# Graph attention on one core: the planner of the instruction order models two lines of transfers instead of one, with other durations and latencies

## The chip, the cores and the metric

The kernel runs on one core of a Trainium2 chip. The metric is the device time of one execution in microseconds (us). The engines that matter here are TensorE (matmuls, "PE" in the profile; "PEld" is its loading of weights), VectorE ("DVE"), ScalarE ("ACT"), GpSimd ("POOL") and SyncE ("SP"). SyncE only issues DMA transfers. GpSimd issues the accumulating transfers. Every engine works through its own list of instructions in order, and waits at the head of the list for semaphores of the others.

## What is computed

32 graphs of 512 nodes with 512 features each go through a layer norm with ReLU, two layers of graph attention (4 heads of 256, then one head of 512) and a residual:

```
h = relu(layernorm(x));  mask = (adj > 0) | eye
def gat(x, W, a_src, a_dst, bias):
    xl = (x @ W) per head
    e = leaky_relu(<xl, a_src>[source] + <xl, a_dst>[target], 0.2);  e = where(mask, e, -1e9)
    return einsum(softmax(e over sources), xl) + bias
out = x + gat2(elu(gat1(h)))
```

All data are float32; the masks inside the kernel are bfloat16.

## The kernel before, in words

**Tiles and stages.** A graph's 512 rows lie as four blocks of 128 partitions. A graph passes these stages: load of x in four blocks (`load`), load of adj and making of the mask (`masks`), layer norm (`norm`, `norm_turn`), projection of layer 1 (`project1`), attention weights of each head (`Soft.columns`, `first`, `second`), their product with the projected features (`gather1`), projection of layer 2 (`project2`), the attention of layer 2 in the same way (`second_layer`, `gather2`), and the store. Most products are done with seven half-size products in place of eight, so VectorE forms sums of blocks (`sums`, `sums1`, `sums2`) before a product and combines results after it. The main loop (line 1429) interleaves stages of several graphs.

**Transfers.** On SyncE's queue (issued at line 448 unless said): blocks of x and adj (256 KB each), the residual's x and the outputs (512 KB), the mask's copy to memory (dm<-m), the mask's transposes (mt<-m, line 603) and, for graphs from the third on, the transposes of normalised x (x<-adj, line 662). Each row of scores goes through memory: `lay` writes a small flipped block (drr<-flip, das<-flip) and `spread` reads it back to all partitions (rr<-drr, as<-das, up to 512 KB). On GpSimd's queue (line 453) the mask is added to the scores p by accumulating transfers (p<-dm, two of 512 KB for a head), and GpSimd also computes a power for the layer norm (line 622).

**A head's chain.** VectorE writes p from rr (four instructions, line 445), two accumulates add the mask, ScalarE takes exp of p (four instructions, line 442), VectorE forms sums of p, TensorE multiplies (line 459). There are three slots for p, two each for rr, as and adj. In `norm_turn`, ScalarE copies a block of x into a slot of adj (adj<-x), SyncE transposes it back into x (x<-adj), and ScalarE writes ht from it.

**The order.** Everything is first recorded as jobs (`Program.add`): engine, cost in us, keys that it reads and writes, and for a transfer its size in us of the memory path. `order` then makes a list schedule by a model of the engines. TensorE's jobs keep the order in which they were recorded; the order on the other four engines is what the planner chooses: each time the job that can start first, and among an engine's ready ones the one with the lowest rank. Ranks come from a pass from the end backwards (`backwards`), twelve rounds of backward and forward passes, and then a local search (`sooner`), which raises jobs that stand behind a modelled hole of TensorE. `emit` writes the instructions out in the order found. The modelled times are used for nothing else.

**Transfers in the model before.** There is one line of transfers for both queues. A transfer starts 0.8 us after its issue ends (`DMA_LEAD`) or when the line is free, takes its size, and its readers are released 2.0 us later (`DMA_TAIL`); SP and POOL are held while the line is over 3.5 us ahead (`AHEAD`):

```
landed = max(landed, t + jobs[j][1] + self.DMA_LEAD) + jobs[j][4]
r = landed + self.DMA_TAIL
```

The issue of a transfer costs 0.4 us on SP (1.3 for a transpose, 0.55 for a flip) and 0.95 on POOL.

Of the kernel before, what the change touches and what calls it, by code (L numbers as in the profile page):

```python
# [19 lines left out]
P = 128  # L20
# [80 lines left out]
class Program:  # L101
# [6 lines left out]

    CROSS, SAME = 0.15, 0.07
    PAIRS = {("PE", "ACT"): 0.21, ("PE", "DVE"): 0.21, ("DVE", "POOL"): 0.58, ("POOL", "DVE"): 0.4}  # L110
    DMA_LEAD, DMA_TAIL, AHEAD = 0.8, 2.0, 3.5

    def __init__(self):
        self.jobs, self.writer, self.readers = [], {}, defaultdict(list)
# [25 lines left out]
    def forwards(self, rank):  # L140

        jobs, after = self.jobs, self.after
        n = len(jobs)
        cause = [None] * n
        left = [len(job[2]) for job in jobs]
        ready_at, start, landed = [0.0] * n, [0.0] * n, 0.0
        free, soon, ready = defaultdict(float), defaultdict(list), defaultdict(list)
        tensor = deque(j for j in range(n) if jobs[j][0] == "PE")
        for j in range(n):
            if not left[j] and jobs[j][0] != "PE":  # L150
                heappush(soon[jobs[j][0]], (0.0, j))
        done = []
        while len(done) < n:
            j, t = self.next_job(rank, free, soon, ready, tensor, left, ready_at, landed - self.AHEAD)
            start[j] = t
            free[jobs[j][0]] = t + jobs[j][1]
            done.append(j)
            if jobs[j][4] is not None:
                landed = max(landed, t + jobs[j][1] + self.DMA_LEAD) + jobs[j][4]
            for s in after[j]:  # L160
                if jobs[j][4] is not None:
                    r = landed + self.DMA_TAIL
                else:
                    r = t + jobs[j][1] + self.latency(j, s)
                if r > ready_at[s]:
                    ready_at[s], cause[s] = r, j
                left[s] -= 1
                if not left[s] and jobs[s][0] != "PE":
                    heappush(soon[jobs[s][0]], (ready_at[s], s))
        return start, done, cause  # L170

    def sooner(self, rank, start, cause, span, gain, first, last):
# [16 lines left out]
    def backwards(self, rank):  # L189

        jobs = self.jobs
        n = len(jobs)
        left = [len(s) for s in self.after]
        ready_at, start, moving = [0.0] * n, [0.0] * n, 0.0
        free, soon, ready = defaultdict(float), defaultdict(list), defaultdict(list)
        tensor = deque(j for j in reversed(range(n)) if jobs[j][0] == "PE")
        found = [j for j in range(n) if not left[j]]
        todo = n
        while True:
            for j in found:  # L200
                if jobs[j][4] is not None:
                    moving = max(moving, ready_at[j]) + jobs[j][4]
                    ready_at[j] = moving + self.DMA_LEAD
                if jobs[j][0] != "PE":
                    heappush(soon[jobs[j][0]], (ready_at[j], j))
            if not todo:
                return start
            j, t = self.next_job(rank, free, soon, ready, tensor, left, ready_at)
            start[j] = t
            free[jobs[j][0]] = t + jobs[j][1]  # L210
            todo -= 1
            found = []
            for d in jobs[j][2]:
                later = self.DMA_TAIL if jobs[d][4] is not None else self.latency(d, j)
                ready_at[d] = max(ready_at[d], t + jobs[j][1] + later)
                left[d] -= 1
                if not left[d]:
                    found.append(d)

    def next_job(self, rank, free, soon, ready, tensor, left, ready_at, hold=0.0):  # L220

        best = None
        for e in ("PE", "ACT", "DVE", "POOL", "SP"):
            if e == "PE":
                if not tensor or left[tensor[0]]:
                    continue
                t = max(free[e], ready_at[tensor[0]])
            elif ready[e]:
                t = free[e]
            elif soon[e]:  # L230
                t = max(free[e], soon[e][0][0])
            else:
                continue
            if e in ("SP", "POOL"):
                t = max(t, hold)
            if best is None or t < best[0]:
                best = (t, e)
        t, e = best
        if e == "PE":
            return tensor.popleft(), t  # L240
        while soon[e] and soon[e][0][0] <= t:
            k = heappop(soon[e])[1]
            heappush(ready[e], (rank[k], k))
        return heappop(ready[e])[1], t

    ROUNDS = 12

    def order(self):
        jobs = self.jobs
# [5 lines left out]

        need, pe = [0.0] * n, None
        for j in reversed(range(n)):
            later = self.DMA_LEAD + self.DMA_TAIL + (jobs[j][4] or 0.0)
            need[j] = max(
                (  # L260
                    need[s] + jobs[s][1] + (later if jobs[j][4] is not None else self.latency(j, s))
                    for s in self.after[j]
                ),
                default=0.0,
            )
            if jobs[j][0] == "PE":
                if pe is not None:
                    need[j] = max(need[j], need[pe] + jobs[pe][1])
                pe = j
# [43 lines left out]
def tile_gat(  # L313
# [254 lines left out]
    def load(b):  # L568
        XT[b] = []
        for t in range(NT):  # L570
            xk, xt = xs.take()
            dma(0.75, (), [xk], xt, x[b, t * P : (t + 1) * P, :])
            XT[b].append((xk, xt))

    def masks(b):

        MASK[b] = mk, md = mds.take()
        tk, mt = mts.take()
        every = [("m", t) for t in range(2)]
        for g in range(2):  # L580
            for t in range(2):
                ak, a = adjs.take()
                row = (2 * g + t) * P
                dma(0.75, (), [ak], a, adj[b, row : row + P, :])
                dve(
                    0.34, [ak], [("m", t)], nc.vector.tensor_scalar,
                    m[:, t, :], a, 0.0, -BIG, op0=OP.is_le, op1=OP.mult,
                )
                adjs.give(ak)
            blocks = bass.AP(  # L590
                tensor=m.tensor, offset=m.offset + 2 * g * P, ap=[m.ap[0], [N + P, 2], [1, P]]
            )
            dve(
                0.3, every, every, nc.vector.tensor_max,
                blocks, blocks, diag[:, None, :].to_broadcast([P, 2, P]),
            )
            dma(
                0.25, every, [mk + (g,)],
                md[:, 2 * g : 2 * g + 2].rearrange("p t n -> p (t n)"), m.rearrange("p t n -> p (t n)"),
            )  # L600
            prog.add(
                "SP", 1.3, every, [tk + (g,)],
                lambda g=g: nc.sync.dma_start_transpose(
                    mt[:, 2 * g : 2 * g + 2].rearrange("p t d r -> p (t d) r"),
                    m.rearrange("p t n -> p (t n)"),
                ),
                1.25,
            )
        MASKT[b] = tk, mt

# [20 lines left out]
    def norm_turn(b, t):  # L631
# [19 lines left out]
        else:  # L651
# [10 lines left out]
                lambda: nc.sync.dma_start_transpose(  # L662
                    back.rearrange("p (g n) -> p g n", n=P), words
                ),
                1.27,
            )
            act(
                1.21, [xk], [("ht", t, 0), ("ht", t, 1)],
# [13 lines left out]
    class Soft:  # L682
# [7 lines left out]
        def lay(self, v, keys, rows, through, n=NT):  # L690
# [7 lines left out]
                f, bass.AP(tensor=v.tensor, offset=v.offset, ap=[v.ap[0], [1, k], [0, c]]),  # L698
            )
            dma(  # L700
                0.03, [fk], [dk], dr[:k].rearrange("k (b j) -> b k j", j=32),
                bass.AP(
                    tensor=f.tensor, offset=f.offset, ap=[[c * f.ap[0][0], P // c], [1, 32]]
                ),
# [5 lines left out]
        def spread(self, laid, to):  # L710

            dk, dr, rows, n, through = laid
            ok, o = to.take()
            dma(
                0.18 * rows * n, [dk], [ok], o[:, :rows, : n * P],
                bass.AP(tensor=dr.tensor, offset=dr.offset, ap=[[0, P], [n * P, rows], [1, n * P]]),
            )
            through.give(dk)
            return ok, o
# [73 lines left out]
        def second(self, h):  # L793
# [9 lines left out]
            for d0, d1, laid in self.rr.pop(h):  # L803
# [17 lines left out]
                if not here:  # L821
                    mk, md = MASK[self.b]
                    for us in (0, 1), (2, 3):
                        keys = p_keys(pk, us)
                        accumulate(
                            2.2, keys + [mk + (us[0] // 2,)], keys,
                            *(t[:, us[0] : us[-1] + 1].rearrange("p t n -> p (t n)") for t in (p, md)),
                        )
                for u in range(NT):
# [408 lines left out]
    def residual(b, places=(pair(ts_),) * 2):  # L1238

        XR[b] = []  # L1240
        for r in range(2):
            ks, xr, give = places[r]()
            halves = [*ks, *(("xr", b, r, c) for c in range(2))]
            if len(ks) == 1:
                halves += [ks[0] + (q,) for q in range(2)]
            dma(
                1.5, [x2_key(b, 0, 0)], halves, xr,
                x[b, r * 2 * P : (r + 1) * 2 * P, :].rearrange("(m p) f -> p m f", p=P),
            )
            XR[b].append((ks, halves, xr, give))  # L1250
# [29 lines left out]
    def gather2(b, soft, blocks, order=LAST):  # L1280
# [4 lines left out]
        def put(n, us, bks, ps, fresh):  # L1285
# [9 lines left out]
            if n == 4 or r == 0 and upper[0] == 0:  # L1295
                upper[0] = -1
                dma(
                    1.5, halves, halves,
                    out[b, r * 2 * P : (r + 1) * 2 * P, :].rearrange("(m p) f -> p m f", p=P), xt,
                )  # L1300
                give()
# [9 lines left out]
    def gather2_plain(b, soft):  # L1311
# [3 lines left out]
        for d in range(NT):  # L1315
# [9 lines left out]
            xr = xr[:, d % 2, :]  # L1325
            key = ("xr", b, d // 2, "d", d % 2)
            dve(0.6, [bk, *halves], [key], nc.vector.tensor_add, xr, ps, xr)
            dma(0.75, [key], (), out[b, d * P : (d + 1) * P, :], xr)
            banks.give(bk)
            yield  # L1330
        give_p(pk)
# [191 lines left out]
```

## Time and profile before

| | us |
|---|---|
| median of 3 runs | 2848.57 (2844.51 to 2850.7) |
| the profiled execution | 2833.14 |
| its span, first to last instruction | 2831.3 |
| TensorE busy | 2765.0 |
| VectorE busy | 2432.6 |
| ScalarE busy | 2389.0 |
| GpSimd busy | 327.3 |

The profile is of one execution. Busy times count the time in which an engine has an instruction in work; instructions of one engine overlap a little. In a line of the timeline stand the start, the duration, the engine, the line of the code, the operation, what it writes and reads (buffer numbers left out), the shapes and the number of instructions merged; in brackets the engine's idle time before it, and what ended that. In a line of waits stand the waiting engine and what it waited for, the total in us, the number of times and the longest. DMA share is the mean busy share of the 16 DMA engines; packets of the two queues that overlap on an engine count twice, so it can exceed 1. The granted clock is TensorE's, 1.00 being full speed.

### The profile page before, as it was taken

Reading aid. Unit: us, or ns where it says so; the run is one execution under the profiler, and the core shown is the slowest. Engines: PE = TensorE matmul, PEld = TensorE weight load, DVE = VectorE, ACT = ScalarE, POOL = GpSimd, SP = SyncE. Lnnn points to the kernel's source line nnn. Section 1 sums busy time; section 2 is a strip of 40 time slices with the busy share of each in tenths; the row PEclk is TensorE's granted clock in tenths of the full one; section 3 lists DMA queues with packets and bytes.
Section 4 is the critical chain, followed back from the end, with each engine's and each line's share of the span. In section 5 each row is a group of like instructions: output and inputs, shape, how many; then the busy total and the mean of one; then the engine's idle time right before and its main releaser. Section 6 shows DMA issues by size and latency. Waiting matters only on the chain. (4 is left out here: it accounts for less than half of the span.)

```text
span 2831.3 us, 39738 instructions
## 1 busy us (share of the span) xinstructions
PE 2765.0 (98%) x12524; PEld 2384.8 (84%) x12524; DVE 2432.6 (86%) x5526; ACT 2389.0 (84%) x4506; POOL 327.3 (12%) x356
## 2 busy tenths in 40 slices
PE   8899999999999999999999999999999999999998
PEld 6588888888888888887888878888888888888876
DVE  7788898897888988987888879898888888898885
ACT  5888888888888889887898878988988888888873
POOL 0101111110111101110011101111010111010110
PEclk9999999999999999999999999999999999999999
DMA  7656766668776667776678765677666877666753
GB/s 229 139 142 173 205 186 181 160 181 172 200 189 161 178 181 191 203 176 145 176 183 195 192 144 174 178 211 190 171 166 169 189 186 187 170 178 182 190 168 101
DMA packets 373830, 501.95 MB, mean 177 GB/s; under 512 B 220788, under 2 KB 225652, under 8 KB 373620
## 3 DMA queue, kind: packets, MB, share of 16 engines
q1 hardware_dynamic: 327828, 332.67, 43.0%
q0 software_dynamic: 45792, 166.74, 25.8%
q8 instruction: 99, 1.62, 0.2%
q14 instruction: 111, 0.91, 0.1%
HBM read 316.41 MB, written 51.31 MB: 130 GB/s over the span
## 5 line engine op out<-in xcount | busy, mean ns | idle before, releaser
L459 PE MATMUL mm<-w_sb,hs 128*128 128x257 f32 (+2 forms) x3032 | 695.7, 381 | 1.4 <-DVE hs L445 1.3
L459 PEld LDWEIGHTS mm<-w_sb,hs 128*128 128x128 f32 x3032 | 575.3, 190 | 86.6 <-DVE hs L445 3.8
L459 PE MATMUL mm<-w_sb,ht 128*128 128x258 f32 x2112 | 500.6, 382 | 5.2 <-DVE xl L445 2.4
L459 PE MATMUL mm<-p,xl 128*128 128x256 f32 (+1 forms) x1984 | 485.6, 388 | 20.0 <-ACT p L442 17.5
L445 DVE CUSTOM_DVE_ANT_1 l<-l,mt 128x512 f32<-128x512 f32 x640 | 424.6, 684 | 80.7 <-ACT l L442 75.7
L442 ACT ACTIVATE l<-l,low 128x512 f32<-128x512 f32 x640 | 455.1, 713 | 39.7 <-DVE low L445 37.9
L442 ACT ACTIVATE l<-as,z 128x512 f32<-128x512 f32 x640 | 433.9, 711 | 59.0 <-DMA as<-das 58.3
L442 ACT ACTIVATE p<-p,z 128x512 f32<-128x512 f32 (+1 forms) x636 | 426.9, 709 | 66.8 <-DMA p<-dm 53.1
L453 POOL DMA_DIRECT2D p<-dm x314 | 274.1, 883 | 1653.7 <-DVE p L445 744.0
L459 PE MATMUL mm<-w_sb,h 128*128 128x257 f32 x2048 | 457.4, 381 | 3.4 <-ACT mm L442 3.4
L459 PEld LDWEIGHTS mm<-w_sb,ht 128*128 128x128 f32 x2112 | 401.6, 190 | 63.6 <-DVE xl L445 3.2
L459 PEld LDWEIGHTS mm<-p,xl 128*128 128x128 f32 x1984 | 381.9, 193 | 84.7 <-ACT p L442 22.1
L445 DVE SCALAR_TENSOR_TENSOR p<-rr,z 128x512 f32<-128x512 f32 (+1 forms) x636 | 445.2, 741 | 7.5 <-DMA rr<-drr 6.5
L459 PEld LDWEIGHTS mm<-w_sb,h 128*128 128x128 f32 x2048 | 389.5, 190 | 61.5 <-ACT mm L442 4.2
L442 ACT ACTIVATE xl<-mm 128x514 f32<-128x514 f32 (+2 forms) x380 | 222.5, 586 | 63.4 <-PE mm L459 61.5
L459 PE MATMUL mm<-xl,p 128*128 128x256 f32 (+1 forms) x1024 | 249.2, 386 | 4.7 <-DVE t L445 2.6
L459 PE MATMUL mm<-t,hs 128*128 128x256 f32 x992 | 239.2, 388 | 13.6 <-ACT mm L442 8.8
L459 PEld LDWEIGHTS mm<-t,hs 128*128 128x128 f32 x992 | 191.3, 195 | 45.7 <-ACT mm L442 12.1
L459 PEld LDWEIGHTS mm<-xl,p 128*128 128x128 f32 x1024 | 193.5, 189 | 40.4 <-issue 5.7
L445 DVE SCALAR_TENSOR_TENSOR h<-h,b_sb,xr 128x512 f32<-128x512 f32 x248 | 181.7, 743 | 16.7 <-ACT xr L442 16.5
L442 ACT ACTIVATE xr<-h,b_sb 128x512 f32<-128x512 f32 x248 | 171.9, 715 | 21.0 <-DVE h L445 16.5
L445 DVE TENSOR_TENSOR xl<-xl,mm 128x516 f32<-128x516 f32 (+1 forms) x189 | 129.6, 687 | 48.3 <-PE mm L459 47.0
(110 smaller groups left out, 3215.4 us busy)
## 6 DMA issues: line engine op xcount, KB each, us to landing
p<-dm POOLq DMA_DIRECT2D x314, 512.0 KB, 6.3
rr<-drr SPq DMA_DIRECT2D x159, 512.0 KB
x<-in_x_dram SPq DMA_DIRECT2D x128, 256.0 KB
adj<-in_adj_dram SPq DMA_DIRECT2D x128, 256.0 KB
as<-das SPq DMA_DIRECT2D x64, 512.0 KB
t<-in_x_dram SPq DMA_DIRECT2D x62, 512.0 KB
out_dram<-t SPq DMA_DIRECT2D x60, 512.0 KB
dm<-m SPq DMA_DIRECT2D x64, 256.0 KB
```

What stands on the lines that cost most here:

```text
L442: prog.add("ACT", cost, reads, writes, lambda: nc.scalar.activation(*a, **k))
L445: prog.add("DVE", cost, reads, writes, lambda: f(*a, **k))
L453: lambda: nc.gpsimd.dma_start(to, at, accum_op=OP.add), size,
L459: f(*a, **k)
```

## The change

The forward pass models two lines, SP's and POOL's. A line alone moves at speed 1; while both move, SP's goes at 0.62 and POOL's at 0.70. The transfer starts 0.6 us after its issue ends on SP, and 0.5 us before it ends on POOL; its readers are released 1.0 us after its end. The hold of 3.5 us counts for each line by itself: `behind` is the work that stands in it. The sizes of transfers are new: 1.1 for 0.75 (blocks of x and adj), 2.1 for 1.5 (residual, outputs), 1.9 for 1.25 and 1.27 (transposes), 0.6 for 0.25 (dm<-m), 0.2 for 0.03 (flips), 0.26 for 0.18 a row (rr, as), 2.5 for 2.2 (accumulates). The sizes of the weights' loads stay. The backward pass keeps one line, with the new leads, tail and sizes. `next_job` is divided into finding an engine and time, and `take`.

```diff
-    DMA_LEAD, DMA_TAIL, AHEAD = 0.8, 2.0, 3.5
+    DMA_LEAD, DMA_TAIL, AHEAD = {"SP": 0.6, "POOL": -0.5}, 1.0, 3.5
+    ALONE, SHARED = {"SP": 1.0, "POOL": 1.0}, {"SP": 0.62, "POOL": 0.7}
...
+        wires, now, behind = {"SP": deque(), "POOL": deque()}, 0.0, {"SP": 0.0, "POOL": 0.0}
...
+        def step(until):
+
+            nonlocal now
+            busy = [q for q in wires if wires[q] and wires[q][0][1] <= now]
+            speed = self.SHARED if len(busy) == 2 else self.ALONE
+            event, which = until, None
+            for q in wires:
+                if wires[q]:
+                    j, since, todo = wires[q][0]
+                    t = now + todo / speed[q] if q in busy else since
+                    if t < event:
+                        event, which = t, q
+            for q in busy:
+                wires[q][0][2] -= (event - now) * speed[q]
+                behind[q] -= (event - now) * speed[q]
+            now = event
+            if which in busy:
+                j = wires[which].popleft()[0]
+                release(j, lambda s: event + self.DMA_TAIL)
+            return which is not None
+
+        while len(done) < n:
+            hold = {q: now + behind[q] - self.AHEAD for q in wires}
+            found = self.next_job(rank, free, soon, ready, tensor, left, ready_at, hold, now)
+            if step(found[0] if found else float("inf")):
+                continue
+            t, e = found
+            j = self.take(e, t, rank, soon, ready, tensor)
...
+            if jobs[j][4] is not None:
+                wires[e].append([j, free[e] + self.DMA_LEAD[e], jobs[j][4]])
+                behind[e] += jobs[j][4]
+            else:
+                release(j, lambda s: t + jobs[j][1] + self.latency(j, s))
...
-            dma(0.75, (), [xk], xt, x[b, t * P : (t + 1) * P, :])
+            dma(1.1, (), [xk], xt, x[b, t * P : (t + 1) * P, :])
...
-                1.25,
+                1.9,
...
-                1.27,
+                1.9,
...
-                            2.2, keys + [mk + (us[0] // 2,)], keys,
+                            2.5, keys + [mk + (us[0] // 2,)], keys,
```

More of the change, by code (lines that the diff above doesn't have):

```diff
@@ L145, in forwards @@
         left = [len(job[2]) for job in jobs]
-        ready_at, start, landed = [0.0] * n, [0.0] * n, 0.0
+        ready_at, start = [0.0] * n, [0.0] * n
         free, soon, ready = defaultdict(float), defaultdict(list), defaultdict(list)
         tensor = deque(j for j in range(n) if jobs[j][0] == "PE")
+        wires, now, behind = {"SP": deque(), "POOL": deque()}, 0.0, {"SP": 0.0, "POOL": 0.0}
         for j in range(n):
@@ L152, in forwards, with release @@
         done = []
[L153 to L159, printed above, removed]
+        def release(j, at):
             for s in after[j]:
[L161 to L164, printed above, removed]
+                r = at(s)
                 if r > ready_at[s]:
@@ L169, in forwards @@
                     heappush(soon[jobs[s][0]], (ready_at[s], s))
+        def step(until):
[24 more added lines that the diff above has]
+            j = self.take(e, t, rank, soon, ready, tensor)
+            start[j] = t
+            free[e] = t + jobs[j][1]
+            done.append(j)
+            if jobs[j][4] is not None:
[3 more added lines that the diff above has]
+                release(j, lambda s: t + jobs[j][1] + self.latency(j, s))
         return start, done, cause
@@ L202, in backwards @@
                     moving = max(moving, ready_at[j]) + jobs[j][4]
-                    ready_at[j] = moving + self.DMA_LEAD
+                    ready_at[j] = moving + self.DMA_LEAD[jobs[j][0]]
                 if jobs[j][0] != "PE":
@@ L207, in backwards @@
                 return start
-            j, t = self.next_job(rank, free, soon, ready, tensor, left, ready_at)
+            t, e = self.next_job(rank, free, soon, ready, tensor, left, ready_at)
+            j = self.take(e, t, rank, soon, ready, tensor)
             start[j] = t
@@ L218, in backwards, with next_job @@
                     found.append(d)
-    def next_job(self, rank, free, soon, ready, tensor, left, ready_at, hold=0.0):
+    def next_job(self, rank, free, soon, ready, tensor, left, ready_at, hold={}, now=0.0):
         best = None
@@ L233, in next_job, with take @@
                 continue
-            if e in ("SP", "POOL"):
-                t = max(t, hold)
+            t = max(t, hold.get(e, 0.0), now)
             if best is None or t < best[0]:
                 best = (t, e)
-        t, e = best
+        return best
+    def take(self, e, t, rank, soon, ready, tensor):
         if e == "PE":
-            return tensor.popleft(), t
+            return tensor.popleft()
         while soon[e] and soon[e][0][0] <= t:
@@ L243, in next_job @@
             heappush(ready[e], (rank[k], k))
-        return heappop(ready[e])[1], t
+        return heappop(ready[e])[1]
     ROUNDS = 12
@@ L257, in order @@
         for j in reversed(range(n)):
-            later = self.DMA_LEAD + self.DMA_TAIL + (jobs[j][4] or 0.0)
+            later = self.DMA_LEAD.get(jobs[j][0], 0.0) + self.DMA_TAIL + (jobs[j][4] or 0.0)
             need[j] = max(
@@ L583, in masks @@
                 row = (2 * g + t) * P
-                dma(0.75, (), [ak], a, adj[b, row : row + P, :])
+                dma(1.1, (), [ak], a, adj[b, row : row + P, :])
                 dve(
@@ L597, in masks @@
             dma(
-                0.25, every, [mk + (g,)],
+                0.6, every, [mk + (g,)],
                 md[:, 2 * g : 2 * g + 2].rearrange("p t n -> p (t n)"), m.rearrange("p t n -> p (t n)"),
@@ L700, in lay @@
             dma(
-                0.03, [fk], [dk], dr[:k].rearrange("k (b j) -> b k j", j=32),
+                0.2, [fk], [dk], dr[:k].rearrange("k (b j) -> b k j", j=32),
                 bass.AP(
@@ L714, in spread @@
             dma(
-                0.18 * rows * n, [dk], [ok], o[:, :rows, : n * P],
+                0.26 * rows * n, [dk], [ok], o[:, :rows, : n * P],
                 bass.AP(tensor=dr.tensor, offset=dr.offset, ap=[[0, P], [n * P, rows], [1, n * P]]),
@@ L1246, in residual @@
             dma(
-                1.5, [x2_key(b, 0, 0)], halves, xr,
+                2.1, [x2_key(b, 0, 0)], halves, xr,
                 x[b, r * 2 * P : (r + 1) * 2 * P, :].rearrange("(m p) f -> p m f", p=P),
@@ L1297, in put @@
                 dma(
-                    1.5, halves, halves,
+                    2.1, halves, halves,
                     out[b, r * 2 * P : (r + 1) * 2 * P, :].rearrange("(m p) f -> p m f", p=P), xt,
@@ L1327, in gather2_plain @@
             dve(0.6, [bk, *halves], [key], nc.vector.tensor_add, xr, ps, xr)
-            dma(0.75, [key], (), out[b, d * P : (d + 1) * P, :], xr)
+            dma(1.1, [key], (), out[b, d * P : (d + 1) * P, :], xr)
             banks.give(bk)
```

## The prediction

> **What bounds the kernel now.** I read the page's busy times and slices first, then start, middle and end as three stretches (columns: stretch, length, busy us of TensorE, weight loads, VectorE, ScalarE, GpSimd with instructions, granted clock, DMA share, GB/s).
>
> ```profile
> span 2831.3 us, 39738 instructions
> PE 2765.0 (98%) x12524; PEld 2384.8 (84%) x12524; DVE 2432.6 (86%) x5526; ACT 2389.0 (84%) x4506; POOL 327.3 (12%) x356
> PE   8899999999999999999999999999999999999998
> ```
> ```profile
> 0.00:240.00 240.00, 212.57 (x861) 165.63 (x862) 192.01 (x547) 181.36 (x346) 27.21 (x33) 0.96 0.68 175
> 240.00:2698.00 2458.00, 2431.60 (x11156) 2123.89 (x11155) 2145.43 (x4772) 2137.81 (x4013) 289.79 (x311) 1.00 0.70 180
> 2698.00:2831.30 133.30, 120.84 (x510) 95.25 (x509) 95.13 (x209) 69.86 (x150) 10.35 (x12) 1.00 0.47 139
> ```
>
> TensorE sets the time, and the change can't touch its work: the planner keeps TensorE's own order. Only its holes can change: 27.4 us in the start (240 − 212.6), 26.4 us in the 2458 us of the middle, 12.5 us at the end. The order of the other engines and of two DMA queues decides the middle. There, TensorE's timeline has ten gaps over 0.15 us. Four are large, before 658.4 (4.74), 1346.9 (7.86), 1697.7 (6.61) and 2219.7 (3.18), together 22.4 us; the other six add 3.5 us. Two of the four:
>
> ```profile
> 654.41 1.33 ACT L442 ACTIVATE p<-p,z 128x512 f32<-128x512 f32 x2 [5.46 <-DMA p<-dm]
> 658.41 3.78 PE L459 MATMUL mm<-t,hs 128*128 128x256 f32 x8 [4.74 <-ACT mm L442]
> 661.99 3.17 PE L459 MATMUL mm<-p,xl 128*128 128x256 f32 x8
> 665.00 1.89 PE L459 MATMUL mm<-p,hs 128*128 128x256 f32 x8
> ```
> ```profile
> 1343.14 1.06 ACT L442 ACTIVATE adj<-x 128x1024 uint16<-128x1024 uint16 x1 [11.13 <-DMA x<-adj]
> 1346.88 3.78 PE L459 MATMUL mm<-p,xl 128*128 128x256 f32 x8 [7.86 <-ACT p L442]
> ```
>
> ScalarE, in order, stands behind a transfer: once an accumulate of the mask (p<-dm), once a transpose (x<-adj). TensorE runs dry, and then eight matmuls take 3.78 us instead of 1.89: its granted clock is halved for a while. Half clock adds 1.9 + 1.3 us after the first gap (3.78 and 3.17 against 1.89) and about 1.9, 2.2 and 1.7 us after the others (half the time from their start to where the clock record returns), 9.0 in all. So the four events cost 22.4 + 9.0 = 31.4 us, 7.85 each, and the middle 35 us.
>
> Why the transfers were late is seen in stretches of 2 us around the first event (last two columns: DMA share, GB/s), in the landings of all accumulates, and in the long chain:
>
> ```profile
> 640.00:642.00 2.00, 2.00 (x10) 1.73 (x10) 1.99 (x7) 2.00 (x5) 0.00 (x0) 1.00 1.12 310
> 650.00:652.00 2.00, 2.00 (x11) 1.74 (x11) 0.27 (x1) 0.00 (x0) 0.00 (x0) 1.00 1.23 62
> ```
> ```profile
> DMA to landing us min/median/max: 4.1/6.2/16.2
> ```
> ```profile
> 2113.07 11.71 DMA p<-dm
> 2201.70 15.12 DMA p<-dm
> ```
>
> The two lines can move 310 GB/s together, but with transposes beside accumulates they fall to 62, the engines no less busy. From the packets, a transpose of x without an accumulate beside it takes 1.4 us first packet to last (median of 49); overlapped by over 4 us of accumulates, 5.9 (18 of them, longest 10.1). All four gaps are such jams.
>
> **The change, part by part.** No instruction or DMA is added or removed; costs of compute stay. What moves is the order on ACT, DVE, SP and POOL. I put old and new rules beside the trace, from the issue's start to the reader's release:
>
> Accumulate (POOL): old 0.95 + 0.8 + 2.2 + 2.0 = 5.95, its twin behind it 8.15. New 0.95 − 0.5 + 2.5 + 1.0 = 3.95 alone, twin 6.45; with SP beside it at 0.70, 2.5/0.7 = 3.57: 5.02 and 8.59. Trace: 4.1 / 6.2 / 16.2. Applying both rules to the trace's own issue times (310 accumulates after 100 us), the old promises 0.4 us later than the landing on average and is too early for 85, the new 1.0 us earlier and too early for 233.
>
> Row load (rr, as): old 0.4 + 0.8 + 1.44 + 2.0 = 4.64; new 4.08 alone, 5.35 shared (2.08/0.62); trace median 4.6 from the packets. Block load of x: 3.95 old, 3.1 or 3.77 new, trace 3.05. Transpose of x: 5.37 old; 4.8 or 5.96 new; trace 5.0, worst 15. Flip: 3.38 old, 2.35 new, trace 1.7. The new rules are nearer for lone SP transfers and worse for accumulates.
>
> For the long transposes neither rule sees the jam: for the accumulate at 638.41 that took 15.97 the old rule gives 9.7, the new 7.3; for that at 1326.50 (14.0) 7.8 and 5.1. So the change gives the planner no reason to keep transposes away from accumulates.
>
> Two rules of the Trainium skill speak here. "DMA: Bandwidth & Descriptors", section "Issuing engines are not separate DMA queues", says that transfers of any issuer interleave on the same 16 engines and several issuers save issue time only. That speaks against lines of 0.62 + 0.70 = 1.32 together: at 0.5 each the twin would take 0.45 + 10 + 1 = 11.5 us instead of 8.6. The windows say 310 GB/s in good stretches, where one accumulate alone (0.52 MB in about 2.35 us) is 223, so 1.3 is right there; in the jam 62 makes it 0.3. "Advanced Engine Details and Errata", section "X-Bar Transpose (TRN2)", says that transposes are as fast as ordinary DMAs; by that 1.25 and 1.27 should become the 1.1 of a block load of the same 262 KB, not 1.9. The packets give 1.89 us of all 16 engines against 0.77 for the block load. Measurement decides: 1.9 is right on average, and wrong in a jam.
>
> Backward ranks: these still put all transfers on one line, at the new sizes. A steady batch has on SP 5 rr, 2 + 1 half as, 8 flips, 4 x, 4 adj, 2 dm, 4 + 2 transposes, 2 residuals, 2 outputs: 31.1 us old, 47.0 new; 10 accumulates 22 and 25. Together 53 and 72 of the batch's 86.4 us of TensorE (2765/32): line load 61% to 83%. Transfers and what feeds them get earlier deadlines, so reads stand further ahead of need. That is the gain's mechanism: a late landing then meets slack. Its bounds: at best all four events go (−31.4) and the small gaps too (−3.5), and then the 1.1 us gaps would be the largest left; on the other side, an early transfer holds one of few slots (3 of p, 2 of rr, as and adj) longer and can hold up the next: as many events more, +31.4. I take half the events gone, −15.7, since landings stay as long as before and only part of them meets new slack.
>
> Forward optimism adds waits: an exp placed by a promised landing 1.4 us earlier than before waits at ScalarE's head; behind it are the evictions that free TensorE's banks, and VectorE's sums. Now:
>
> ```profile
> ACT p L442 <- DMA p<-dm: 53.1, 44, 5.5
> ```
>
> 44 waits could become 44 × 233/85 = 121, at 1.2 us 145 us; ScalarE's idle 442 us (2831 − 2389) can hold that. 44 waits come with 3.5 us of small TensorE gaps, so 121 cost at most 3.5 × 77/44 = +6 us; at least below zero, since an exp that stands ready runs the moment its data land. I take +3, nearer to zero because ScalarE's short waits hardly show on TensorE now. Without that cover all 92 us of new wait (145 − 53) would show.
>
> Holds: the old rule held SP and POOL together when the joint line was 3.5 us ahead, the new holds each line by itself, so SP's queue is no longer planned to pause behind accumulates. The power on POOL (line 622) is passed by accumulates or passes them; 0.12 of POOL is busy, and TensorE never waits for it in the middle: 0. Start and end: the start's first 12 us are loads and a normalisation that no order shortens; its later gaps (111 to 229 us) may shift by ±5; I take 0.
>
> **How it may go.** A, fewer jams meet an empty cover: two of four events remain, −15.7 + 3 = −12.7 us: profiled 2833.14 (span 2831.3 plus 1.8) to 2820.4. The runs' median lies 15.4 us above the profiled run, which this profile doesn't explain; I carry the difference over: 2848.57 − 12.7 = 2835.9. For: earlier ranks. Against: the jams are unseen.
>
> B, slower: the plan trusts accumulates, lets SP run beside them, and two more jams reach TensorE: +15.7 + 5 = +20.7, 2869. For: 22 accumulates took over 9.5 us but only four events opened large gaps, so others are near; 233 late promises. It decides where gaps over 3 us number more than four.
>
> C, it does nothing that counts: coincidences fall elsewhere but as often, the waits are hidden: 2848, within 0.2% (5.7 us, about what can be told from no change).
>
> **The numbers.** A, faster by over 0.2%: 0.55. C: 0.14. B: 0.31. A's own range is 2813 (all 35 us of the middle gone) to 2842; the whole range reaches to B's 2870. The forecast is A's 2836.
>
> **What would show it.** Right: TensorE's busy time within a few us of 2765 less the lost half clock, its gaps over 3 us in the middle two or fewer, ScalarE's waits for p<-dm between 44 and 121, and SP's transfers issued earlier before their readers. Wrong: five or more large gaps after transposes and accumulates, each with 3.78 us for eight matmuls behind it; or many gaps of about 1 us in every batch from exps waiting; or the start's holes growing past 33 us.

## The result and the profile after

The changed kernel took 2826.15 us (median of 5 runs, 2822.80 to 2830.66) against 2848.57 for the kernel before on the same chip (5 runs, 2840.23 to 2850.70): a ratio of 0.9927, 95% interval 0.9908 to 0.9946, or 22.4 us. The profiled executions stand closer: 2833.14 before, 2826.34 after.

The page of the changed kernel, and then its three stretches, cut as before:

```profile
span 2824.6 us, 39689 instructions
...
PE 2763.9 (98%) x12524; PEld 2376.7 (84%) x12524; DVE 2432.9 (86%) x5526; ACT 2381.3 (84%) x4506; POOL 328.3 (12%) x356
```
```profile
0.00:240.00 240.00, 213.33 (x862) 165.67 (x863) 194.27 (x551) 179.84 (x344) 25.74 (x32) 0.95 0.67 177
240.00:2698.00 2458.00, 2437.30 (x11191) 2122.85 (x11190) 2153.82 (x4794) 2138.08 (x4031) 292.92 (x313) 1.00 0.69 180
2698.00:2824.60 126.60, 113.29 (x475) 88.20 (x473) 84.80 (x183) 63.38 (x134) 9.67 (x12) 1.00 0.47 133
```

TensorE's work is the same. Its holes (stretch less busy time) in the start are 26.7 us (27.4 before) and in the middle 20.7 (26.4). But the middle's holes are of another kind. Before, four gaps over 3 us made 22.4 of them; now the longest is 2.21 us, and 21 gaps of 0.2 to 2.2 us make the sum. The clock is granted at half for 10.2 us of the middle instead of 23.9. Two rows show what came and what went: ScalarE's wait for accumulates (before: 53.1 us, 44 times) and the landing of accumulates (before: 4.1/6.2/16.2).

```profile
ACT p L476 <- DMA p<-dm: 100.6, 68, 9.9
```
```profile
DMA to landing us min/median/max: 4.1/5.6/12.5
```

The latest landings went, and ScalarE nevertheless waits twice as long for accumulates. One of the new small gaps, in the timeline of the changed kernel; the end of the transfer is in its long chain below:

```profile
1177.96 0.72 ACT L476 ACTIVATE p<-p,z 128x512 f32<-128x512 f32 x1 [2.48 <-DVE p L479]
...
1178.58 1.32 ACT L476 ACTIVATE ht<-x 128x1024 uint16<-128x1024 uint16 x1
...
1179.94 0.69 DVE L479 TENSOR_TENSOR hs<-ht 128x512 f32<-128x512 f32 x1 [2.06 <-ACT ht L476]
...
1180.68 2.67 PE L493 MATMUL mm<-w_sb,hs 128*128 128x258 f32 x8 [2.21 <-DVE hs L479]
```
```profile
1169.19 8.68 DMA p<-dm
1180.68 161.54 PE mm L493 x736
```

ScalarE stands idle 2.48 us before an exp of p. The row names VectorE, but the accumulate issued at 1169.19 landed 8.68 us later, at 1177.87, just before the exp starts at 1177.96: the transfer ended the wait. Behind the exp in ScalarE's order stands ht<-x, behind that VectorE's sum, behind that TensorE, 2.21 us late. In a second profile of the changed kernel the same place grew to a large gap, the only one over 3 us there: a transpose was moving beside the two accumulates, which landed 9.7 and 12.1 us after their issue.

```profile
1178.25 0.72 ACT L476 ACTIVATE p<-p,z 128x512 f32<-128x512 f32 x1 [2.83 <-DMA p<-dm]
1180.98 1.66 PE L493 MATMUL mm<-w_sb,hs 128*128 128x258 f32 x3 [4.28 <-DVE hs L479]
```

### The profile page after: what moved, and what is told of

Read it like the earlier page. It is cut to its first block, busy times and chain, and to the rows that moved or that the text cites. A ratio compares the mean times of both kernels' runs of the same rounds, so it can differ in the third digit from the quotient of the medians.

```text
span 2824.6 us, 39689 instructions
## 1 busy us (share of the span) xinstructions
PE 2763.9 (98%) x12524; PEld 2376.7 (84%) x12524; DVE 2432.9 (86%) x5526; ACT 2381.3 (84%) x4506; POOL 328.3 (12%) x356
## 4 chain that ended last, share of the span: by engine, by line
PE 49%; DMA 4%; ACT 3%; DVE 2%; issue 1%; ACTq 0%; DVEq 0%; POOLq 0%
PE mm L493 49%; DMA p<-dm 2%; ACT l L476 1%; DMA x<-adj 1%; DMA drr<-flip 1%; DVE p L479 1%; ACT p L476 0%; DMA rr<-drr 0%; ACT ht L476 0%; DVE hs L479 0%; DVE t L479 0%; ACT adj L476 0%; ACT xl L476 0%; ACT x L476 0%; ACT mm L476 0%
## 5 line engine op out<-in xcount | busy, mean ns | idle before, releaser
L476 ACT ACTIVATE p<-p,z 128x512 f32<-128x512 f32 (+1 forms) x636 | 433.4, 711 | 122.2 <-DMA p<-dm 100.6
L493 PE MATMUL mm<-p,xl 128*128 128x256 f32 (+1 forms) x1984 | 478.6, 384 | 1.9 <-ACT xr L476 0.8
L479 DVE SCALAR_TENSOR_TENSOR p<-rr,z 128x512 f32<-128x512 f32 (+1 forms) x636 | 454.0, 740 | 30.8 <-DMA rr<-drr 28.2
L476 ACT ACTIVATE l<-l,low 128x512 f32<-128x512 f32 x640 | 454.5, 712 | 20.5 <-DVE low L479 19.8
L476 ACT ACTIVATE h<-mm 128x512 f32<-128x512 f32 (+1 forms) x256 | 146.4, 572 | 30.1 <-PE mm L493 29.5
```

Source lines behind the costliest of these rows:

```text
L476: prog.add("ACT", cost, reads, writes, lambda: nc.scalar.activation(*a, **k))
L479: prog.add("DVE", cost, reads, writes, lambda: f(*a, **k))
L493: f(*a, **k)
```

## The experiments

The runs come in five groups, each on one chip with the kernel before beside it. Only ratios are compared between groups, since the kernel before itself took 2849 us in the first and 2823 to 2827 in the later ones. "Overlapped transposes" below are those of x that ran beside accumulates for over 4 us, summed over the accumulates and counted from the packets; "late accumulates" are those that landed over 9.5 us after their issue, counted after the first 100 us.

### Is the profiled run of before typical?

The kernel before, unchanged (no diff).

> The kernel before, unchanged, profiled once more. If the profiled execution of before (2833 us) was a lucky one, with fewer jams of transposes and accumulates than usual, this profile has five to eight gaps of TensorE over 3 us in the middle and a time near 2848. If the jams are fixed by the order alone, it has the same four gaps at the same places and the 15 us between the profiled run and the median come from elsewhere (the clock, the profiler).

The median of its 12 runs was 2828.87 (2813.95 to 2835.91, the slowest being the profiled one), 1.002 of the same kernel's other runs on that chip (1.0003 to 1.0036): that is how far two equal kernels lie apart. TensorE's waits in the middle, in the second profile:

```profile
PE mm L459 <- ACT p L442: 20.2, 5, 11.9
PE mm L459 <- ACT mm L442: 8.5, 5, 4.0
```

Three gaps over 3 us: 11.90 before 1602.7, 5.16 before 1695.4, 4.04 before 2220.4. Two are near places of the first profile (1697.7 and 2219.7), those near 658 and 1347 are gone and one is new. So neither expectation held; it looks as if the order makes jams possible at certain places, and the execution decides which of them grow. 16 transposes were overlapped (18 in the first profile), 20 accumulates late (22).

### Are transposes what jams?

In both kernels, with each one's order kept, the transposes of x become plain copies, so that these two kernels leave a step of the computation out:

```diff
-                lambda: nc.sync.dma_start_transpose(
-                    back.rearrange("p (g n) -> p g n", n=P), words
-                ),
+                lambda: nc.sync.dma_start(back, words),
```

> The kernel before with its order unchanged, but the 120 transposes of x are issued as plain copies of the same 262 KB (so the second layer's input is not transposed). If the transposes beside the accumulates make the jams, all gaps over 3 us in the middle go and the time falls by 25 to 45 us, to 2805 to 2823. If the accumulates or the sum of traffic make them, the gaps stay and the time moves by less than 8 us.

> The changed kernel with its order unchanged, the 120 transposes of x as plain copies in the same way. If the change gained by keeping jams away from TensorE, little is left to gain: 0 to 8 us below 2826, so 2818 to 2826. If it gained by something else and has its jams still, it falls as much as the kernel before does, by 25 us or more.

(What stays untransposed is the first layer's input of the graphs from the third on, not the second layer's input as the first of these texts has it.) The kernel before fell to 2792.17, a ratio of 0.9888 (0.9873 to 0.9903), 31.0 us below the 2823.19 of before on that chip; the changed kernel's order gave 2799.69, 0.9916 (0.9901 to 0.9930). The middle of the first and of the second:

```profile
240.00:2698.00 2458.00, 2456.13 (x11321) 2145.64 (x11320) 2183.29 (x4856) 2163.52 (x4069) 296.09 (x319) 1.00 0.64 183
```
```profile
240.00:2698.00 2458.00, 2450.38 (x11290) 2139.56 (x11289) 2175.09 (x4849) 2152.51 (x4063) 297.31 (x318) 1.00 0.64 182
```

With copies of the same bytes in the same places, TensorE's holes in the middle are 1.9 us in the old order and 7.6 in the new, and no gap is over 3 us. The large gaps need the transposes. A copy is also lighter (DMA share 0.64 for 0.70), so this run alone doesn't tell the meeting from the weight. The new sizes on one line, below, help: all 120 transposes are there, one is overlapped, and no gap is over 3 us, so the weight alone makes no large gap.

Without transposes the changed kernel's order is the slower one, by 7.5 us (0.9916 against 0.9888), so its gain over before goes with the jams. Whether its rules cost the 7.5 us isn't shown: two orders under equal rules lie as far apart (next section). I had expected little left to gain in the changed order. Its ratio falls from 0.9927 in one group and 0.9968 in another to 0.9916, and its holes fall from 20.7 to 7.6 us, though its order and promises are the same and ScalarE still waits:

```profile
ACT p L476 <- DMA p<-dm: 80.2, 54, 9.7
```

So most of the small gaps need the transposes too. By this pair of runs, an early promise costs TensorE less where transfers are not slowed as well.

### Rules, or a draw?

```diff
-    DMA_LEAD, DMA_TAIL, AHEAD = 0.8, 2.0, 3.5
+    DMA_LEAD, DMA_TAIL, AHEAD = 0.8, 2.0, 3.6
```

> The kernel before with the hold at 3.6 us in place of 3.5: a change of no meaning that draws another order. If the order's gains are a draw (which transfers happen to meet), this moves by 10 us or more in either direction. If the old rules as such cost the time, it stays within 8 us of 2848.

1.0053 (1.0036 to 1.0070), 13 us above before, with 12 overlapped transposes, 18 late accumulates, and gaps of 4.78, 3.97 and 5.10 us. The same edit in the changed kernel, and the changed kernel once more:

> The changed kernel with the hold at 3.6 us in place of 3.5, a change of no meaning that draws another order. If the new rules avoid jams as a rule, it has no gap over 3 us in the middle and lies within 8 us of the changed kernel. If the changed kernel's order is a lucky draw, it has two to four such gaps again and lies 10 us or more above it.

> The changed kernel, unchanged, beside the kernel before on the chip of this call. The kernel before took 2849 us in one call and 2823 in another. If the change's gain is its avoided jams, and jams differ from chip to chip, the ratio to before moves with before: at 2823 for before the changed kernel gains 0 to 10 us, at 2848 about 22. If the gain is the order as such, the ratio is 0.993 again.

The changed kernel: 2815.36 (22 runs) against 2826.90, 0.9968 (0.9950 to 0.9987). Its other draw: 2826.41 (14 runs), 0.9999 (0.9973 to 1.0024), 11 us above the changed kernel, though its profile has no gap over 3 us. That profile is of its fastest execution (2810.54 of 2810.54 to 2843.58), so it may show fewer gaps than most have. So orders under the same rules lie 0.3 to 0.5% apart, and the changed rules' gain is of that size. Yet the counts don't overlap:

| | overlapped transposes | late accumulates | transposes whose first packet came with 3 or more accumulates issued and not landed |
|---|---|---|---|
| before, its repeat, its other draw | 18, 16, 12 | 22, 20, 18 | 15, 15, 9 |
| changed, its repeat, its other draw | 5, 6, 5 | 8, 9, 7 | 0, 0, 0 |

All counts are of 120 transposes and 306 accumulates. The thinning of jams belongs to the rules; what it is worth in time differs by draw. Between chips I expected the ratio to move with before; it did (0.9927 at 2849, 0.9968 at 2827), but two groups prove little.

### Sizes or lines?

The new sizes on the old single line, with its lead and tail, and the old sizes on the two new lines, with theirs (shown for one of the eleven sizes of the first edit; the second is its reverse):

```diff
-                1.27,
+                1.9,
```

> The kernel before with the changed kernel's sizes of transfers, still on one line with the old lead and tail. If the sizes (the longer transposes above all) are what thins out the jams, gaps over 3 us in the middle fall to one or none and the time is near the changed kernel's, 10 us or more below before. If the two lines are what does it, it stays with three or more such gaps and within 8 us of before.

> The changed kernel with the old sizes, on two lines with the new leads and tail. If the sizes are what thins out the jams, they come back: two or more gaps over 3 us in the middle and 8 us or more above the changed kernel. If the two lines do it, it stays near the changed kernel.

Both are slower: 1.0188 (1.0158 to 1.0218) and 1.0624 (1.0594 to 1.0655). Both also have few overlapped transposes (1 and 3), so each half thins the jams by itself (one order each). Each half has its own price. The new sizes on one line, TensorE's waits:

```profile
PE mm L459 <- DVE t L445: 16.6, 25, 1.9
PE mm L459 <- ACT p L442: 12.2, 11, 3.4
PE mm L459 <- ACT w_sb L442: 12.0, 3, 8.0
```

46 gaps of at most 2.53 us in the middle (34.0 us), and larger holes in the start (32.6 us for 27.4) and at the end (21.9 for 12.5): the line that the planner believes in is 83% full by the prediction's sum, which fits a plan that puts off transfers; I didn't try that by itself. ScalarE waited for accumulates only 20 times (13.5 us). The old sizes on two lines are the opposite: the plan believes that transfers are quick and parallel, ScalarE waits for accumulates 130 times, and TensorE has 121 gaps of 117.7 us in the middle, three of them over 3 us.

```profile
ACT p L476 <- DMA p<-dm: 260.8, 130, 9.7
```

Neither of my theories was right: for the time, sizes and lines need each other.

### Is it the backward pass?

The changed kernel, with the old sizes, lead and tail in `backwards` alone:

```diff
+    WAS = {1.1: 0.75, 2.1: 1.5, 1.9: 1.26, 0.6: 0.25, 0.2: 0.03, 2.5: 2.2, 2.08: 1.44, 1.04: 0.72}
...
-                    moving = max(moving, ready_at[j]) + jobs[j][4]
-                    ready_at[j] = moving + self.DMA_LEAD[jobs[j][0]]
+                    size = round(jobs[j][4], 2)
+                    moving = max(moving, ready_at[j]) + self.WAS.get(size, size)
+                    ready_at[j] = moving + 0.8
...
-                later = self.DMA_TAIL if jobs[d][4] is not None else self.latency(d, j)
+                later = 2.0 if jobs[d][4] is not None else self.latency(d, j)
```

> The changed kernel, but its backward pass keeps the old sizes (0.75, 1.5, 1.26, 0.25, 0.03, 1.44, 2.2), lead 0.8 and tail 2.0; the forward pass is the changed one. If the fuller backward line (83% for 61%) is what draws transfers apart, as the prediction has it, the jams return: twelve or more transposes overlapped by over 4 us of accumulates, two or more gaps over 3 us, and the ratio to before is 1.00 or above. If the forward pass does it, there are six or fewer, and the ratio stays 0.99 to 1.00.

The ratio was 1.0050 (1.0031 to 1.0069), as if the backward pass were the source; but only 5 transposes were overlapped. ScalarE waits for accumulates 79 times (127.1 us). Gaps in the middle are 24.1 us, two over 3 us (3.49, 4.81), and 12 accumulates were late, none over 12 us. So, in this order, the forward pass keeps transposes from accumulates without the fuller backward line. Why this order is 0.8 to 1.2% behind the changed kernel's ratios, when draws alone differ by 0.3 to 0.5%, is not settled: the fuller backward line may be worth time by another way.

### The early promise of accumulates

```diff
-    DMA_LEAD, DMA_TAIL, AHEAD = {"SP": 0.6, "POOL": -0.5}, 1.0, 3.5
+    DMA_LEAD, DMA_TAIL, AHEAD = {"SP": 0.6, "POOL": 0.9}, 1.0, 3.5
```

> The changed kernel with GpSimd's lead at +0.9 us in place of -0.5, so that an accumulate is promised 1.4 us later, 5.35 us after its issue when alone. If the early promises cost small waits, ScalarE's waits for accumulates fall from 64 to 68 of about 95 us to about 45 of 55 us, TensorE's gaps under 3 us in the middle from 17 to 20 us to 10 or less, and the time by 5 to 10 us. If they are harmless, gaps and time stay within 4 us.

The backward pass uses the same lead, so accumulates also get deadlines that are 1.4 us earlier; the run doesn't separate the two. 2801.70 (11 runs) against 2826.57: 0.9917 (0.9891 to 0.9943). ScalarE's waits, then the middle stretch, of this kernel:

```profile
ACT p L476 <- DMA p<-dm: 28.5, 20, 9.7
```
```profile
240.00:2698.00 2458.00, 2454.86 (x11313) 2148.44 (x11311) 2178.27 (x4849) 2158.66 (x4065) 299.60 (x317) 1.00 0.69 183
```

Waits fell from 68 and 64 to 20, below the old rule's 44. TensorE's holes in the middle fell to 3.1 us, from 20.7 and 21.3, with jams no rarer (6 overlapped transposes, 9 late accumulates). To see whether that was a draw:

```diff
-    DMA_LEAD, DMA_TAIL, AHEAD = {"SP": 0.6, "POOL": -0.5}, 1.0, 3.5
+    DMA_LEAD, DMA_TAIL, AHEAD = {"SP": 0.6, "POOL": 0.9}, 1.0, 3.6
```

> The kernel with the later promise (GpSimd's lead +0.9) and the hold at 3.6 us in place of 3.5: another order under the same rules. If the later promise is what closes the small gaps, the middle has 10 us of gaps or less and 20 to 40 of ScalarE's waits for accumulates again, and the ratio to before is 0.988 to 0.996. If the 0.9917 of the later promise was a draw, the gaps are back at 16 to 24 us and the ratio near 0.997 to 1.005.

2810.08 (6 runs) against 2825.45: 0.9949 (0.9929 to 0.9969). Its waits and TensorE's, in the middle:

```profile
ACT p L476 <- DMA p<-dm: 36.9, 28, 9.6
```
```profile
PE mm L493 <- DVE hs L479: 12.9, 4, 3.4
PE mm L493 <- ACT xl L476: 0.9, 3, 0.5
```

Half of what I expected came: waits are 28, in the expected range, but the holes are 13.9 us. Four gaps of 2.98, 3.19, 3.38 and 3.33 us, 88 us apart at 492, 581, 669 and 758, make 12.9 of them: one place of the order that repeats in four graphs. I didn't follow it further. In both draws the later promise lies 0.5% below the early one (0.9917 against 0.9968, 0.9949 against 0.9999), but the changed kernel's 0.9927 of the first group lies between the two. The changed kernel and these never ran on one chip together; through before, the first of them is, narrowly, the fastest of the tried orders that compute the whole function.

### Can the planner see the jam?

```diff
+            if len(busy) == 2 and jobs[wires["SP"][0][0]][4] == 1.9:
+                speed = {"SP": 0.3, "POOL": 0.4}
```

> The changed kernel whose forward pass also prices the jam: while a transpose stands at the head of SP's line and an accumulate moves, the lines go at 0.3 and 0.4 in place of 0.62 and 0.70. If the planner can keep them apart once it sees the price, three or fewer transposes are overlapped by over 4 us of accumulates, no gap is over 3 us, and the ratio to before is 0.985 to 0.993. If the list schedule can't use it, since transfers meet by what happens on the chip, it stays at 0.993 to 1.002.

1.0024 (1.0008 to 1.0040). Three transposes were overlapped, so the price may be heeded, but the middle has 21.6 us of gaps, one of 5.32, the start 33.7 in place of 25 to 27, and ScalarE waits for accumulates as in the changed kernel (103.9 us, 63 times). In this one order a price for the jam bought nothing beside the early promise.

## Why the prediction was right or wrong

**What bounds the kernel: right.** The jams of transposes and accumulates were priced at 31.4 us from four events; taking transposes away from the old order gave 31.0 us and left no large gap. That these are so close is partly luck, since the second profile's jams fell elsewhere.

**"So the change gives the planner no reason to keep transposes away from accumulates": wrong.** The rule doesn't price a jam, that much is so, but its orders have 5 or 6 overlapped transposes where the old ones have 12 to 18. The step that failed is the comparison of rules at the trace's own issue times: it tests what a rule promises for an old order, and not which order the rule makes. What the new order no longer has is the accumulates of two heads together around a transpose (15 transposes began with three or more in flight, then none).

**The backward line as the gain's mechanism: fell.** Transfers were to be issued earlier before their readers, so that late landings meet slack. With issues and readers of the middle paired in order, the mean distance from issue to reader is (the rows of as are left out):

| us | before | changed |
|---|---|---|
| transposes of x to ht | 14.6 | 12.0 |
| loads of adj to the mask | 15.4 | 13.5 |
| accumulates to exp | 10.1 | 8.3 |
| rows (rr) to p | 7.8 | 8.3 |

Only the rows gained, by half a microsecond; the other three stand nearer to their readers, in the repeats and other draws too. So the late landings became fewer, and, rows aside, they did not meet more slack. With the old backward pass, transposes stay apart as well; for the time, the backward pass's part is open (1.0050). The thinning comes with either half of the change, sizes or lines; that the halves must stand together to gain time was not in the prediction at all.

**The optimism term: right in mechanism, mis-sized.** Waits were to rise from 44 to at most 121, and rose to 68 (100.6 us, 1.5 us each). That the exps stand 1.8 us nearer to their accumulates (table above; 9.2 and 9.6 us with the later promise) is the optimism itself. I took +3 us for TensorE and at most +6; the small gaps rose by 17.0. The later promise, with its earlier deadlines, took away 18 us of holes in one draw (21 to 3), 2 in the other (16.1 to 13.9), and 0.5% of the time, some 14 us, in both. In the second draw the holes say little, since the two profiled executions took the same time (2810.54 and 2810.55). And the term isn't the promise alone: with copies for transposes the small gaps shrink to 7.6 us under the same promises. The error was to scale the six small gaps of before by the number of waits. What stands behind a wait decides: in the timeline above it is ht<-x, and in the changed kernel's repeat VectorE's sums (hs), which read ht, end 14.6 of the 21 us that TensorE waits in the middle; none of the four large gaps of before ended so.

```profile
PE mm L493 <- DVE hs L479: 14.6, 8, 4.3
```

**A reading of the two lines.** The 310 GB/s at 640 us was taken to show that two lines carry more than one. The same view has nearly as much at 626 us, before the first accumulate of that stretch (631.14), with SyncE's transfers alone:

```profile
626.00:628.00 2.00, 2.00 (x11) 1.76 (x10) 2.00 (x5) 1.40 (x3) 0.00 (x0) 1.00 0.80 309
```

It shows only that the two together carry more than one accumulate's 223. No run here tests the speeds 0.62 and 0.70 by themselves.

**The sum.** I had half of the events gone and +3: −12.7. In the profiled pair, gaps over 3 us went from 22.4 us to none, the small ones rose from 3.5 to 20.5, and the half clock now costs at most 5.1 us (half of 10.2) instead of 9.0: −22.4 + 17.0 − 3.9 = −9.3 in the middle. Start and end gave some of it back (half clock in the start 23.9 us for 20.5, holes at the end 13.3 for 12.5), and the pair differs by 6.8. So all the large gaps went where half were to go, the small waits cost nearly six times the +3, and that the two errors offset each other is luck. The first group showed 22.4 us, a later one 11.5 (2826.90 to 2815.36). What the first group has beyond the profiled pair's 6.8 is not explained: before's five runs there (2840 to 2851) all lie above its profiled execution, and its runs in the later groups lie at 2805 to 2843. The 15.4 us that I carried over unchanged are of the size of that spread.

**The rivals.** B, slower by two jams more, didn't happen; trusting the accumulates did cost time, but by small waits and not by more jams. C, coincidences that fall elsewhere but as often, is wrong for the counts, and yet the changed kernel's other draw stands at 0.9999: for the time of a single draw it wasn't far off.

**What would show it.** ScalarE's waits (68, within 44 to 121) and the large gaps (none, and one in the repeat) came as listed. SyncE's transfers issued earlier before their readers did not. "Many gaps of about 1 us in every batch from exps waiting" was listed as a sign of being wrong, and it came in part: 21 gaps in the middle, fewer than one a batch.

## What to carry to other kernels

In a schedule for engines that work in order, a reader of a transfer that was promised too early blocks everything behind it; here the most trusting model (old sizes on two lines, 1.0624) lost more than the most cautious (new sizes on one line, 1.0188), and both lost. Judge a planner's model by the orders it makes and by at least two draws of each, since a meaningless edit moved the time here by 0.3 to 0.5%. Check the mechanism too, not only the gain: here the jams became rarer, while the earlier issues that were to absorb them did not come. And where transfers jam by chance, one profile shows some of the places that can jam, not which will.

## What the runs showed of the hardware

A transpose of 262 KB with no accumulate beside it took 1.4 us from first packet to last (medians of 49 and 63, before and after); over 4 us beside accumulates made it 5.9 us (18 of them), up to 12.4 in the second profile of before, while accumulates took up to 16.2 us to land (20.7 in that second profile). Plain copies of the same bytes in the same order left no accumulate over 12 us (8 before) and five over 9.5. The kernel before ran at medians of 2849, 2823, 2827, 2827 and 2825 us in the five groups of runs.
